# Moving stores, token sums and down-weight sums between the stages of a four-layer LoRA kernel, with five rank-table buffers

## The chip, the core and the metric

The kernel runs on one core of one Trainium2 chip. The metric is the device time in microseconds (us) of one execution. The core has five engines with a stream of instructions each: PE (matrix products; PEld is its weight load), DVE and ACT (elementwise work; both can read and write PSUM, where products arrive), POOL (elementwise work on SBUF, and indirect gathers), and SP, which here only issues transfers. ACT and POOL issue transfers too. Each stream is worked off in its order.

## The reference

Eight sequences of 256 tokens with 1024 features pass four layers, each added to its input. Every sequence b picks its own low-rank (rank 16) adapter in each layer.

```python
# layer 0: dense 1024 -> 1024 with bias, plus adapter times 2
x = x + (x @ W.T + b + 2.0 * (x @ A0[i0[b]]) @ B0[i0[b]])
# layer 1: gate and up 1024 -> 2752, silu, down 2752 -> 1024, adapters times 0.5 on all three
g = x @ W_gate.T + 0.5 * lora(x, A_gate, B_gate, i1[b])
u = x @ W_up.T   + 0.5 * lora(x, A_up, B_up, i1[b])
h = silu(g) * u
x = x + (h @ W_down.T + 0.5 * lora(h, A_down, B_down, i1[b]))
# layers 2 and 3: adapters alone
x = x + (x @ B2[i2[b]].T) @ A2[i2[b]].T
x = x + (x @ B3[i3[b]].T) @ A3[i3[b]].T
```

All of it is float32.

## The kernel before

The 2048 tokens are two blocks of 1024. Features lie on the 128 partitions, tokens along the free dimension. The large products use a seven-product scheme for 2 by 2 block matrices (seven products of sums of blocks in place of eight), once for layer 0 and for the last part of the down projection, and in two levels for the rest, where each of the seven outer products is again made of seven. So sums of weights and sums of tokens are needed next to each product: POOL makes most of the weight sums, DVE and ACT the token sums.

The work is a list of units, in this order: `layer0(0)` and `layer0(1)` with four units each; then for block 0 and after it for block 1 `gate_up` (first `rest()`, a group of leftover columns with seven short units, then five groups 0 to 4 of seven units), the two-level `Down` (seven units, called d_0 to d_6 below) and four units `2_blk_o` of the one-level down products. After the last of these, `last_layers()` applies layers 2 and 3 and stores the outputs. A unit has seven products and slots 0 to 9 between them. Other work is put in with `u.at(slot, f)`, or with `u.before(k, slot, f)` for a slot of the unit k places earlier. There is also a side queue, `beside`, of small work items with a cost: at each slot, items are taken from its front until their costs reach the unit's share. `need(key)` takes items until that key is done, so a unit that needs its token sums drains everything ahead of them.

This gives a program order. The framework then orders each engine's stream by its own planning of what is ready when, with program order as the priority, and sets the semaphores; tiles come from pools, and a load waits for a free tile of its pool.

Names that matter here:

- `upool` has 22 tiles of 1 MB (`big(...)`); nearly all weights, tokens and results lie in them.
- `apool` holds the gathered rank tables: `a0`, `agu` (two for each block, for the gate and up adapters, gathered by `shrink_tables` and copied into `w_r_B` by ACT at L1047), `bb` (for layers 2 and 3) and `a2s`.
- `prepare_tokens(blk, kk, h)` makes one half (kk) of the token sums of layer 1's outer products: four `inner` sets and two `outer_sums`, written to DRAM (`toks`). `load_tok` reads them back as `tk` (`tk_r` for the leftover group).
- `finished(kk)` in layer 0 stores layer 0's result to `x1d`, and calls `prepare_tokens` for block 0. For block 1 this is done later by `next_tokens`, which loads `x1d` as `xn`.
- `sum_down(c)`, c from 0 to 7, makes an eighth of the outer weight sums of the down projection (`wo` to `wsum`), once for both blocks, in POOL's stream.
- `Down.load_first` and `load_second` load a unit's weights (`dw_d`, `dx_d`, `db_d`) and tokens (`dh_d`, `dk_d`); `sum_weights` (POOL, L591 to L594) and `sum_tokens` (DVE and ACT, through PSUM tiles `pt_d`) make the inner sums.
- Results of the outer products are `c_X`, `c_E`, `c_Z`, `c_Y` (`c_d_` in the down stage, `c_r_` in the leftover group); DVE combines two of them at L496. `td` (L927) collects the down adapter's rank rows, and `pl` (L931) are the adapter products of gate and up.

Of the kernel before, what the change touches and what calls it, by code (L numbers as in the profile page):

```python
# [13 lines left out]
P = 128  # L14
# [10 lines left out]
NBLK = NB * S // TB  # L25
NN = TB // 512
# [26 lines left out]
def kernel(  # L53
# [50 lines left out]

    const = ctx.enter_context(tc.tile_pool(name="const", bufs=1))
    upool = ctx.enter_context(tc.tile_pool(name="u", bufs=NBIG))
    apool = ctx.enter_context(tc.tile_pool(name="a", bufs=3))
    adpool = ctx.enter_context(tc.tile_pool(name="ad", bufs=2))
    bpool = ctx.enter_context(tc.tile_pool(name="b", bufs=1))
    bgpool = ctx.enter_context(tc.tile_pool(name="bg", bufs=2))  # L110
# [521 lines left out]

    def prepare_tokens(blk, kk, h):


        t, items = {}, []

        def add(cost, f):
            items.append((cost, f))

        def outer():
            for n in ("sa", "sb"):
                t[n] = big(f"{n}_{blk}_{kk}").rearrange("p (i c t) -> p i c t", i=2, c=2)

        def outer_sums(c):
            a, b = ((h[n][:, 0, c], h[n][:, 1, c]) for n in range(NN))
            held = []

            def start():
                for x in (a, b):  # L650
                    held.append(bank(ps_l, f"pq_{blk}_{kk}_{c}_{len(held)}"))
                    copy(held[-1], x[0])

            def first():
                p1, p2 = held
                nc.vector.tensor_sub(t["sb"][:, 0, c], p1, b[0])
                nc.vector.tensor_add(p2, p2, b[1])

            def second():
                p1, p2 = held  # L660
                copy(t["sa"][:, 0, c], p2)
                nc.vector.tensor_sub(p1, p2, a[0])
                copy(t["sa"][:, 1, c], p1)
                nc.vector.tensor_sub(t["sb"][:, 1, c], a[1], p1)

            return (0, start), (1.4, first), (1.4, second)

        def inner(n, get, place, count):
            def start():
                b = get().rearrange("p i c (j t) -> p i (c j) t", j=2)  # L670
                t[n, "b"] = b
                t[n, "t"] = big(f"tt_{n}_{blk}_{kk}")[:, : count * 1024].rearrange(
                    "p (i s t) -> p i s t", i=count, s=4
                )
                nc.sync.dma_start(
                    out=toks[blk][place : place + count, kk, :, : 3 * S].rearrange("i p t -> p i t"),
                    in_=b[:, :, 1:4, :].rearrange("p i s t -> p i (s t)"),
                )
                b12, b11, b22, b21 = (b[:, :, j, :] for j in range(4))
                t[n] = token_sums(  # L680
                    f"pr_{n}_{blk}_{kk}",
                    b11,
                    b12,
                    b21,
                    b22,
                    *(t[n, "t"][:, :, j, :] for j in range(4)),
                    like=lambda ps: ps[:, : count * S].rearrange("p (i t) -> p i t", i=count),
                )

            def store():  # L690
                nc.sync.dma_start(
                    out=toks[blk][place : place + count, kk, :, 3 * S :].rearrange("i p t -> p i t"),
                    in_=t[n, "t"].rearrange("p i s t -> p i (s t)"),
                )
                ready.update((blk, k, kk) for k in range(place, place + count))

            cost = 0.84 if count == 1 else 1.4
            add(0, start)
            add(0, lambda: t[n][0]())
            add(cost, lambda: t[n][1]())  # L700
            add(cost, lambda: t[n][2]())
            add(0, store)

        inner("h0", lambda: h[0], 0, 2)
        split = len(items)
        add(0, outer)
        for c in range(2):
            items.extend(outer_sums(c))
        inner("sb", lambda: t["sb"], 4, 2)
        inner("sa", lambda: t["sa"], 2, 2)  # L710
        inner("h1", lambda: h[1][:, 1:2], 6, 1)
        return items[:split], items[split:]


    x1d = [
# [26 lines left out]
    def layer0(blk):  # L742
# [63 lines left out]
        def finished(kk):  # L806
            for n in range(NN):
                nc.sync.dma_start(
                    out=x1d[blk][n, kk], in_=st["x1", n, kk].rearrange("p i c t -> p (i c t)")
                )  # L810
            if blk == 0:
                for items in prepare_tokens(blk, kk, [st["x1", n, kk] for n in range(NN)]):
                    beside.extend(items)

        def plain(o, at):

# [64 lines left out]
        for i, o in enumerate((0, 2, 1, 3)):  # L881
            if blk == 0 and i == 0:
                u = Unit("0_plain", lambda at, o=o: plain(o, at), 0)
                u.before(1, 0, lambda o=o: load_w(o))
                u.before(1, 0, load_x)
                for c in range(HC):
                    u.before(1, 0, lambda c=c: sum_x(c))
            else:
                u = Unit(f"0_{blk}_{o}", lambda at, o=o: job(o, at), 1.3)
                u.before(1, 0, lambda o=o: load_w(o))  # L890
                u.before(1, 3, lambda o=o: sum_w(o))
                if i == 0:
                    u.before(1, 0, load_x)
                    for c in range(HC):
                        u.before(1, 4 + c // 2, lambda c=c: sum_x(c))
                    u.at(4, first_shrink)
            if i % 2:
                u.at(8, lambda kk=o % 2: finished(kk))

    def gate_up(blk):  # L900
        st = sts[blk]
# [38 lines left out]
        def job(g):  # L940
# [86 lines left out]
            q = Quads(blk, f"1_{blk}_{g}", 2, raw, done, SHARE)  # L1027
            q.units[0].before(3, 0, lambda: tables(g))
            if blk == 0 and g < KQ:
                for s, c in ((2, 2 * g), (5, 2 * g + 1)):  # L1030
                    q.units[s].at(4, lambda c=c: sum_down(c))

        def rest():

# [89 lines left out]
    def down_projection(blk):  # L1124
# [21 lines left out]

            queue(("x2", blk, mh, n), *((0.69, lambda k=k: add(k)) for k in range(HC)))

        Down(blk, f"d_{blk}", done)

        def load_h():
            st["h"] = []
# [154 lines left out]
        def last_layers():  # L1307
# [7 lines left out]
            for o in range(NC):  # L1315
# [3 lines left out]
                for n in range(NN):  # L1319
                    nc.vector.tensor_add(x2[o][n], x2[o][n], pss[n])  # L1320
                    at = blk * TB + n * 512
                    nc.scalar.dma_start(
                        out=outT[o * P : (o + 1) * P, at : at + 512], in_=x2[o][n]
                    )

        def next_tokens():

            parts = []
            for kk in range(2):
                h = []  # L1330
                for n in range(NN):
                    t = big(f"xn_{blk}_{n}_{kk}")
                    nc.sync.dma_start(out=t, in_=x1d[blk + 1][n, kk])
                    h.append(t.rearrange("p (i c t) -> p i c t", i=2, c=2))
                parts.append(prepare_tokens(blk + 1, kk, h))
            for part in zip(*parts):
                for items in part:
                    beside.extend(items)

        for o in range(HC):  # L1340
            u = Unit(f"2_{blk}_{o}", lambda at, o=o: job(o, at), 1.2)
            for g in (KQ, REST):
# [7 lines left out]
                u.before(2, 5, tables23)  # L1350
            else:
                u.at(5, lambda o=o: shrink23([o - 1, o - 1 + HC]))
            if o == 0 and blk + 1 < NBLK:
                u.at(3, next_tokens)
        units[-1].at(9, last_layers)

    for blk in range(NBLK):
# [148 lines left out]
```

## Time and profile before

| | us |
|---|---|
| median of 3 runs | 1838.62 |
| the three runs | 1838.72, 1838.62, 1835.54 |
| profiled execution | 1848.62 |
| its span, from the first to the last instruction | 1846.9 |

| engine | busy us | share of the span | instructions |
|---|---|---|---|
| PE | 1797.9 | 97% | 7588 |
| PEld | 1314.5 | 71% | 7588 |
| DVE | 1082.2 | 59% | 1674 |
| POOL | 1001.2 | 54% | 773 |
| ACT | 308.4 | 17% | 548 |

A row of the profile names the source line, the engine, the operation and the tiles, result first, without their numbers; what stands in brackets is the time that the engine stood idle before it and what ended that. The mean granted clock of PE is 0.989 of full speed. The stages lie in the trace as follows: layer 0 to 243 us, block 0's gate and up to about 768, its two-level down products to about 948, its one-level ones to about 1026, mixed with the first leftover products of block 1 from 1022 on; block 0's last layers end near 1048.

### The profile page before, as it was taken

The numbers are of one execution on the slowest core, as the hardware profiler recorded it, in microseconds if no ns is written. First come the engines' busy times: TensorE is split into PE (matmuls) and PEld (weight loads), VectorE is DVE, ScalarE is ACT, GpSimd is POOL, SyncE is SP. The second block draws the span as 40 slices with busy tenths as digits, with TensorE's granted clock in tenths as the row PEclk, the third lists the DMA queues.
The fourth block names the chain that finished last, engine by engine and source line by source line (L and its number), as shares of the span: only waits on it lengthen the run. The fifth ranks groups of instructions, "written<-read, shape, count | busy, mean of one in ns | idle before, by whom it ended". The sixth has DMA issues, their size and how long they took to land.

```text
span 1846.9 us, 20533 instructions
## 1 busy us (share of the span) xinstructions
PE 1797.9 (97%) x7588; PEld 1314.5 (71%) x7588; DVE 1082.2 (59%) x1674; ACT 308.4 (17%) x548; POOL 1001.2 (54%) x773
## 2 busy tenths in 40 slices
PE   7899999999999999999999699999999999999998
PEld 3344477878788878788864377888888887888843
DVE  3475235676857575755554564656565657456623
ACT  0112013111111112123112132020202030122100
POOL 5102067897988877453520568585858574344400
PEclk9999999999999999999999899999999999999999
DMA  6177466768686857573664884666666656555302
GB/s 225 77 256 297 157 280 235 278 214 313 222 307 239 309 198 266 200 252 120 218 256 142 313 357 152 231 228 231 227 231 230 229 198 243 205 195 179 113 0 91
DMA packets 114707, 402.33 MB, mean 218 GB/s; under 512 B 12336, under 2 KB 42160, under 8 KB 105136
## 3 DMA queue, kind: packets, MB, share of 16 engines
q1 hardware_dynamic: 97920, 362.84, 53.7%
q0 software_dynamic: 10208, 27.67, 4.3%
q10 hardware_dynamic: 6480, 10.51, 1.6%
q8 instruction: 61, 1.00, 0.2%
q14 instruction: 38, 0.31, 0.0%
HBM read 316.56 MB, written 84.41 MB: 217 GB/s over the span
## 4 chain that ended last, share of the span: by engine, by line
PE 88%; DVE 7%; DMA 2%; issue 1%; another core or an unknown queue 1%; POOL 0%; ACT 0%; ACTq 0%; DVEq 0%
PE pa L453 25%; PE pc L453 12%; PE pa_d L453 10%; PE pa L352 9%; PE pb L453 6%; PE pc_d L453 5%; PE pc L352 5%; PE pb_d L453 3%; PE pa_r L453 2%; PE pb L352 2%; PE pl L931 2%; PE pc_r L453 1%; DVE c_Y L496 1%; PE pd L238 1%
## 5 line engine op out<-in xcount | busy, mean ns | idle before, releaser
L453 PE MATMUL pa<-tk,sw 128*128 128x256 f32 x1120 | 270.6, 385 | 1.7 <-DVE c_X L484 1.7
L453 PE MATMUL pc<-tk,sw 128*128 128x256 f32 x1120 | 268.2, 383 | 0.0
L453 PEld LDWEIGHTS pa<-tk,sw 128*128 128x128 f32 x1120 | 210.2, 191 | 59.7 <-issue 14.0
L453 PEld LDWEIGHTS pc<-tk,sw 128*128 128x128 f32 x1120 | 214.8, 192 | 31.4 <-issue 1.6
L453 PE MATMUL pa<-tk,w_B 128*128 128x256 f32 x960 | 228.5, 381 | 0.4 <-DVE c_Y L487 0.4
L453 PEld LDWEIGHTS pa<-tk,w_B 128*128 128x128 f32 x960 | 181.2, 190 | 35.2 <-DVE c_E L484 6.5
L423 POOL TENSOR_TENSOR sw<-w_B 128x512 f32<-128x512 f32 x60 | 76.5, 1275 | 106.9 <-PE pa L453 87.0
L453 PE MATMUL pb<-tk,w_B 128*128 128x256 f32 x480 | 114.2, 381 | 0.0
L591 POOL TENSOR_TENSOR dx_d<-dw_d 128x1024 f32<-128x1024 f32 x14 | 33.4, 2387 | 143.5 <-PE pa L453 44.3
L453 PE MATMUL pa_d<-dh_d,dw_d 128*128 128x256 f32 x448 | 101.3, 379 | 0.0
L453 PE MATMUL pc_d<-dh_d,dw_d 128*128 128x256 f32 x448 | 101.3, 379 | 0.0
L453 PEld LDWEIGHTS pb<-tk,w_B 128*128 128x128 f32 x480 | 92.1, 192 | 12.8
L484 DVE TENSOR_TENSOR c_X<-c_X,pa 128x512 f32<-128x512 f32 x90 | 61.3, 681 | 63.7 <-PE pa L453 63.7
L414 POOL TENSOR_TENSOR w_B<-w_B,w_B 128x1024 f32<-128x1024 f32 x40 | 93.7, 2366 | 2.4 <-PE pa L453 2.4
L453 PEld LDWEIGHTS pa_d<-dh_d,dw_d 128*128 128x128 f32 x448 | 85.1, 190 | 11.6
L453 PEld LDWEIGHTS pc_d<-dh_d,dw_d 128*128 128x128 f32 x448 | 85.1, 190 | 11.6
L425 POOL TENSOR_TENSOR sw<-w_B 128x512 f32<-128x512 f32 x60 | 83.9, 1398 | 0.0
L426 POOL TENSOR_TENSOR sw<-w_B,sw 128x512 f32<-128x512 f32 x60 | 81.8, 1363 | 3.5
L424 POOL TENSOR_TENSOR sw<-sw,w_B 128x512 f32<-128x512 f32 x60 | 80.2, 1336 | 0.0
L263 ACT ACTIVATE c_X<-pa 128x512 f32<-128x512 f32 x30 | 17.8, 592 | 368.9 <-PE pa L453 332.6
L208 POOL DMA_INDIRECT ad<-in_ad_dram,off_a x48 | 45.6, 950 | 27.3 <-PE pd L238 16.4
L352 PE MATMUL pa<-ht,wd 128*128 128x512 f32 x128 | 59.3, 595 | 1.0 <-DVE c_d_Y L1225 1.0
(363 smaller groups left out, 3178.2 us busy)
## 6 DMA issues: line engine op xcount, KB each, us to landing
tk<-toks SPq DMA_DIRECT2D x140, 896.0 KB
w_B<-in_wgu_dram SPq DMA_DIRECT2D x40, 1024.0 KB
tk_r<-toks SPq DMA_DIRECT2D x28, 896.0 KB
hk<-c_Z SPq DMA_DIRECT2D x32, 512.0 KB
dh_d<-hk SPq DMA_DIRECT2D x14, 1024.0 KB
hk<-c_Y SPq DMA_DIRECT2D x24, 512.0 KB
w<-in_w_dram SPq DMA_DIRECT2D x16, 512.0 KB
x1d<-x SPq DMA_DIRECT2D x8, 1024.0 KB
```

The costliest lines, as they stand in the source:

```text
L208: nc.gpsimd.indirect_dma_start(out=t, out_offset=None, in_=table, in_offset=bass.IndirectOffsetOnAxis(ap=off, axis=0),)
L238: nc.tensor.matmul(ps[32 * r : 32 * r + 32, :], v, src, start=start, stop=stop, skip_group_check=True)
L352: nc.tensor.matmul(ps, v[j], m[j], start=start and k == 0, stop=k == len(moving) - 1, skip_group_check=True,)
L414: f(self.raw[out][:, c], self.raw[a][:, c], self.raw[b][:, c])
L423: nc.gpsimd.tensor_add(s1, m21, m22)
L424: nc.gpsimd.tensor_sub(s2, s1, m11)
L425: nc.gpsimd.tensor_sub(s3, m11, m21)
L426: nc.gpsimd.tensor_sub(s4, m12, s2)
L453: nc.tensor.matmul(ps[:, q, :], w(j, q, kk), tok(j, kk), start=start and q == 0 and kk == 0, stop=kk == self.deep - 1, skip_group_check=True,)
L484: nc.vector.tensor_add(view(out, r, k), view(old, r, k), ps)
L591: nc.gpsimd.tensor_sub(s3, a11, a21)
L931: nc.tensor.matmul(ps[outs], st["bgu", g][rows, table, n, cols], st["t"][rows, table, n, :], start=True, stop=True, skip_group_check=True,)
```

## The change

Five things are altered.

- The output stores of block 0 are no longer issued in `last_layers` right after each add; each becomes an item of cost 0.2 in the side queue, where units of block 1's leftover group take them. Block 1's stores stay where they were.
- `next_tokens` is no longer called at slot 3 of the first one-level down unit for both halves; it is called for one half at slot 0 of unit d_1 and for the other at slot 0 of unit d_3 of block 0's two-level down products.
- `prepare_tokens` returns one list in place of two; before, the two halves' lists were interleaved for block 1.
- `sum_down`: the first goes to slot 6 of the third unit of `layer0(1)`, the next two to slot 0 of the fourth, and the other five to groups 0, 0, 1, 1 and 2 of block 0 (two in each of groups 0 to 3 before).
- `apool` has five tiles in place of three.

```diff
-    apool = ctx.enter_context(tc.tile_pool(name="a", bufs=3))
+    apool = ctx.enter_context(tc.tile_pool(name="a", bufs=5))
...
         inner("h0", lambda: h[0], 0, 2)
-        split = len(items)
         add(0, outer)
...
-        return items[:split], items[split:]
+        return items
...
             if blk == 0:
-                for items in prepare_tokens(blk, kk, [st["x1", n, kk] for n in range(NN)]):
-                    beside.extend(items)
+                beside.extend(prepare_tokens(blk, kk, [st["x1", n, kk] for n in range(NN)]))
...
                 u.at(8, lambda kk=o % 2: finished(kk))
+            if blk == 1 and i > 1:
+                for c in ((0,), (1, 2))[i - 2]:
+                    u.at((6, 0)[i - 2], lambda c=c: sum_down(c))
...
             if blk == 0 and g < KQ:
-                for s, c in ((2, 2 * g), (5, 2 * g + 1)):
-                    q.units[s].at(4, lambda c=c: sum_down(c))
+                for s, c in ((2, 2 * g + 3), (5, 2 * g + 4)):
+                    if c < 8:
+                        q.units[s].at(4, lambda c=c: sum_down(c))
...
-        Down(blk, f"d_{blk}", done)
+        two = Down(blk, f"d_{blk}", done)
...
-                    nc.scalar.dma_start(
-                        out=outT[o * P : (o + 1) * P, at : at + 512], in_=x2[o][n]
-                    )
-
-        def next_tokens():
-
-            parts = []
+
+                    def store(o=o, n=n, at=at):
+                        nc.scalar.dma_start(
+                            out=outT[o * P : (o + 1) * P, at : at + 512], in_=x2[o][n]
+                        )
+
+
+                    if blk + 1 < NBLK:
+                        beside.append((0.2, store))
+                    else:
+                        store()
+
+        def next_tokens(kk):
+
+            h = []
+            for n in range(NN):
+                t = big(f"xn_{blk}_{n}_{kk}")
+                nc.sync.dma_start(out=t, in_=x1d[blk + 1][n, kk])
+                h.append(t.rearrange("p (i c t) -> p i c t", i=2, c=2))
+            beside.extend(prepare_tokens(blk + 1, kk, h))
+
+        if blk + 1 < NBLK:
             for kk in range(2):
-                h = []
-                for n in range(NN):
-                    t = big(f"xn_{blk}_{n}_{kk}")
-                    nc.sync.dma_start(out=t, in_=x1d[blk + 1][n, kk])
-                    h.append(t.rearrange("p (i c t) -> p i c t", i=2, c=2))
-                parts.append(prepare_tokens(blk + 1, kk, h))
-            for part in zip(*parts):
-                for items in part:
-                    beside.extend(items)
-
+                two.units[1 + 2 * kk].at(0, lambda kk=kk: next_tokens(kk))
...
-            if o == 0 and blk + 1 < NBLK:
-                u.at(3, next_tokens)
```

## The prediction

> **What bounds the kernel now.** I read the page first: PE is busy in 97% of the span and holds 88% of the chain of work that ended last, so only time in which PE stands, or runs at a lower granted clock, can be won. Of its 40 slices one in the middle stands out with a 6: the hand-over from block 0 to block 1. Stretches of 10 us show it, with one stretch of block 0's gate-up stage below them. The columns are PE, PEld, DVE, ACT and POOL busy time with counts, then granted clock, DMA share and GB/s.
>
> ```profile
> 1010.00:1020.00 10.00, 9.12 (x33) 3.31 (x31) 5.34 (x10) 4.84 (x9) 5.07 (x6) 1.00 0.25 86
> 1020.00:1030.00 10.00, 7.02 (x28) 2.48 (x28) 7.00 (x12) 2.67 (x5) 1.18 (x2) 1.00 0.86 309
> 1030.00:1040.00 10.00, 6.66 (x16) 3.18 (x17) 5.41 (x11) 1.74 (x4) 8.42 (x11) 0.70 0.88 316
> 1040.00:1050.00 10.00, 8.29 (x29) 3.98 (x27) 7.90 (x13) 0.00 (x0) 3.75 (x6) 0.96 1.03 370
> 1050.00:1060.00 10.00, 2.23 (x5) 1.85 (x6) 0.42 (x1) 0.77 (x2) 8.35 (x8) 0.73 1.03 375
> 1060.00:1070.00 10.00, 10.00 (x45) 8.65 (x44) 3.19 (x8) 1.40 (x4) 4.44 (x5) 0.93 1.00 390
> 660.00:670.00 10.00, 8.34 (x22) 5.49 (x20) 7.21 (x11) 0.00 (x0) 10.00 (x7) 0.66 0.83 308
> ```
>
> From 1010 to 1060 PE stands for 16.7 us (0.88 + 2.98 + 3.34 + 1.71 + 7.77). Next, the waits of PE tell who ended these stops (total, times, longest):
>
> ```profile
> PE pc_r L453 <- ACT c_r_X L263: 8.6, 1, 8.6
> ...
> PE pc_r L453 <- POOL sw_r L423: 2.6, 1, 2.6
> PE p L238 <- DVE pq L662: 1.7, 1, 1.7
> ...
> PE pa L352 <- DVE c_d_Y L1225: 1.0, 1, 1.0
> ```
>
> And the timeline tells what those engines were held by. ACT's copy came late because 16 output stores stood ahead of it in ACT's stream; POOL's sums stood behind table gathers that waited for a free buffer; SP took 17.74 us over six token loads.
>
> ```profile
> 1028.52 0.94 POOL L208 DMA_INDIRECT bb<-in_bb_dram,off_a  x1 [8.53 <-PE p L238]
> ...
> 1042.79 17.74 SPq L402 DMA_DIRECT2D tk_r<-toks  x6
> ...
> 1057.24 0.38 ACT L263 ACTIVATE c_r_X<-pc_r 128x256 f32<-128x256 f32 x1 [19.05 <-DMA out_dram<-c_d_Y]
> ...
> 1057.77 2.05 PE L453 MATMUL pc_r<-tk_r,sw_r 128*128 128x256 f32 x4 [8.55 <-ACT c_r_X L263]
> ```
>
> **The change, part by part.** Each gain below is PE standing time plus the clock lost around it.
>
> *Stores.* Before, each of 16 stores (256 KB) is issued by ACT right behind its DVE add; unhindered an issue takes 0.34 us, but from the ninth on ACT also waits for earlier transfers (the chain shows 4.41 us for one), so `c_r_X` comes 19.05 us late and PE stands 8.6 us. After, the stores are side items of cost 0.2 in the first remainder unit of block 1: its share is 0.5 per slot, so three go per slot and all 16 in six slots, with the unit's copies between them. A copy can still meet one waiting store: I leave half of the 4.41 us in the sum. Gain 8.6 - 2.2 = 6.4. If all stores are still ordered ahead of the copies, the gain is 0. The four result tiles (of 22) are freed a few us later; among the waits of SP's queue, token loads already waited 11.0 us for `out_dram<-c_d_Y`. What pays for that is the next part.
>
> *Token sums.* Per half (kk) this moves 20 DVE operations of 0.69 us and 4 of 0.42 = 15.5 us, 20 ACT copies (17 of about 0.6 us, 3 of 0.39: 11.4 us), and 10 transfers (two 1 MB loads, eight stores, 8.1 MB together; SP's issues take about 0.35 us each, 3.5 us). They leave 933 to 1040, where DVE's stream held PE by 1.7 and 1.0 us (the rows above) and 0.3 us more (`c_d_X` L1225), and go beside the down products d_1 and d_3. Gain 3.0. It also makes the first remainder tokens ready 100 us earlier, so that SP's 17.74 us of late loads has no part any more. The cost is in the down stage, where PE never stands now:
>
> ```profile
> 800.00:850.00 50.00, 50.00 (x236) 43.07 (x235) 26.86 (x37) 13.11 (x24) 23.03 (x12) 1.00 0.69 238
> 850.00:900.00 50.00, 50.00 (x234) 44.01 (x233) 27.64 (x40) 12.20 (x21) 19.53 (x13) 1.00 0.48 163
> ```
>
> DVE is busy 27 of 50 us. A down unit is 7 products of 3.45 us = 24.2 us, so DVE has 24.2 x 23/50 = 11 us free in it, and a half needs 15.5. The side queue is first-in first-out and each down unit drains it up to its own token sums: d_2's sums stand behind the whole half. If the half must fit into one unit, they are 4.5 us late, twice: 9 us. On SP, ahead of the second loads of unit d_2 and d_4, two 1 MB loads are put; at the page's mean of 218 GB/s that is 9.6 us, and ACT's first copy waits for them (7.5 and 9.6 us before, `pr_h <- DMA xn`); a PSUM product of 3.45 us covers only part. Bounds 0 and 13 with some clock; below 0 is excluded, since PE has no stop here to lose. I take 3, near the low end, because DVE stands as long as 16.7 us at a time in this stage (before its operation at 859.25), so work that is ready can run early.
>
> *Five rank-table buffers.* The trace has POOL standing 39.6 us before the second `agu` table (for the ACT copies of the first), 3.7 us before the first `bb` and 8.53 us before the second, for the last shrink products of block 0; `sw_r` stands behind that. With five, two `bb` and two `agu` tables of the hand-over fit at once and one is free; the next tables take `agu`'s place after its copies, not `bb`'s. Gain 2.6. The second `agu` gathers (4 of 1.25 us with issue) come about 90 us earlier, among the `wd` sums near 915; POOL stood 7.1 us there, which covers them; without that cover they cost up to 5. Below, the sums keep their durations.
>
> *Clock.* The granted clock was 0.70, 0.96, 0.73 and 0.93 in the four stretches from 1030: (0.30 x 6.7) + (0.04 x 8.3) + (0.27 x 2.2) + (0.07 x 10) = 3.6 us of PE's time, and it goes with the stops. So far 6.4 + 3.0 + 2.6 + 3.6 = 15.6. What stays: about 3.5 us of short stops in block 0's last layers (DVE `t`, `c_d_E`, `c_d_X`) and at `trep`. They are what is late next.
>
> *Down-weight sums.* A `sum_down` is 4 POOL operations of 1.28 us and 5 POOL DMA issues (0.8 and 4 of 0.56), 2 MB in all, in one tile. Eight run now in block 0's gate-up, two in each of four groups; of these the second of group 3 falls on DVE's crowded end:
>
> ```profile
> 655.77 1.28 POOL L423 TENSOR_TENSOR sw<-w_B 128x512 f32<-128x512 f32 x1
> 655.92 4.12 DVE L496 TENSOR_TENSOR c_Y<-c_Y,c_X 128x512 f32<-128x512 f32 x1
> ...
> 661.89 1.99 PE L931 MATMUL pl<-trep,bgu 32*128 32x512 f32 x2 [1.66 <-DVE td L927]
> ```
>
> The `wo` work delayed POOL's `sw` sums into DVE's add of two SBUF tiles, which took 4.12 us where it takes 0.69 alone; DVE's backlog then held PE 1.66 us, and the clock fell to 0.66 in that stretch (0.34 x 8.3 = 2.8). After, group 3 has none and group 2 only its first: gain 1.7 + 2.8 = 4.5. Here a rule speaks otherwise. The Trainium skill ("TensorE: Matmul & The Clock Gate", "The HAM clock gate") has the clock fall only after an idle window of about 3.4 us; by it this stop would cost 1.7 alone and the sum be 2.8 smaller. The row shows the loss after 1.66 us, with 22 matmuls where neighbours have 50, so I take 4.5 and keep 1.7 as the low end. Three sums go to block 1's layer 0 (about 211 to 243 us), where POOL stands 32 us for a buffer. There a rule speaks against the change: by "SBUF — State Buffer", "Who interferes with whom", a DVE operation with two SBUF inputs waits for a GpSimd operation that reads SBUF to finish, and layer 0's weight sums on DVE are of that kind. By the rule that is at most 1.28 us each, by the row above 3.4. DVE is busy 12.6 of 50 us from 200 to 250, so either is hidden. The three tiles are dearer: SP already took 24.4 us over four remainder-token loads at 197. Bounds 0 and 8, none below 0; I take 1, since four tiles of x come free in the same units.
>
> **Sum.** -15.6 - 4.5 + 3 + 1 = -16.1 us. The profiled execution took 1848.6 (span 1846.9), 10.0 above the median of 1838.62, so 1832.5 by its own time and 1822.5 by the median. With the bounds its own range is 1810 to 1831.
>
> **Rivals.** *The stores stay in the way.* The streams are ordered by the framework's planner, which already runs remainder products among the last down products; it may keep 16 stores together, or the kept result tiles may hold the token loads. Then 6.4 and the clock of the last two stretches (1.3) stay lost: -16.1 + 7.7 = -8.4, 1830. For: the stores are ready as soon as DVE is done, whatever their place in the program. Against: the copies would now come first in program order.
>
> *Tiles run out beside the down products: slower.* A down unit asks for 7 of the 22 tiles, and three units overlap, beside up to four result tiles. A half of the token sums asks for 8 more (2 loaded, 2 outer, 4 inner sums). Tiles come free at 7 per 24.2 us, one per 3.45 us. The lead of a unit's last load over its first reader:
>
> ```profile
> 833.80 0.32 SPq L585 DMA_DIRECT2D dk_d<-hk  x1
> ...
> 859.85 0.68 DVE L321 TENSOR_TENSOR dk_d<-dh_d,pt_d 128x512 f32<-128x512 f32 x1
> ```
>
> is 26 us, less some 5 us of transfer: 21. Six tiles held at once delay a load by 6 x 3.45 = 20.7, just within it; with eight it is 27.6 and PE stands 7 us per half. If the second half starts before the first has let go, up to sixteen delay it by 55 and PE stands about 34 us. From 24 us in the down stage the kernel is slower; 7 + 7 is not enough, an overlap is. A partial overlap (11 to 13 tiles, 17 to 24 us on top of one half's 7) gives 1838.6 - 19.1 + 28 = 1847.5; the full one 1853. For: loads already go out only when tiles come free, at the pace of the units. Against: the halves are two units (48 us) apart.
>
> **How the numbers follow.** The sum as worked out: 0.53. Stores still in the way: 0.18. Gains and down-stage cost about equal: 0.05. Tiles short: 0.24. Anything within 0.2% (3.7 us) counts as no change, about what a measurement of this kernel can tell. So faster 0.70, same 0.06 (it takes in a tail of the second case), slower 0.24. The range runs from 1806 (the remaining short stops gone too) to 1848 (through the partial overlap), which leaves out about 0.05 below and 0.12 above.
>
> **What would show it.** Right: no row of PE waiting for ACT `c_r_X` over 3 us, stores between ACT copies, no POOL wait of 39.6 us at `agu`, `xn` loads near 790 and 840, `tk_r` loads before 1000, clock 1.00 across the hand-over, no stop near 660. Wrong: PE below 49 of 50 us between 790 and 910 with `pa_d` or `pc_d` waiting for DVE `pt_d` or POOL `dw_d`; ACT standing behind stores as now; a stop at 243 to 300 for `tk_r`. A down stage longer by over 20 us would overturn the forecast.

## The result and the profile after

The changed kernel takes 1823.9 us (median of 19 runs, 1816.38 to 1836.04) against 1836.95 for the kernel before (19 runs beside it): ratio 0.9938, with a 95% interval of 0.9922 to 0.9954, so 8 to 14 us less (the ratio is taken over all timed runs; the two medians alone would give 0.9929). The profiled execution took 1823.25 us, span 1821.5.

The same stretches of 10 us around the hand-over (PE, PEld, DVE, ACT, POOL busy with counts, then granted clock, DMA share, GB/s), and the three stretches that the prediction showed of gate-up and down:

```profile
1010.00:1020.00 10.00, 10.00 (x35) 3.73 (x34) 2.58 (x4) 0.38 (x1) 0.00 (x0) 1.00 0.26 93
1020.00:1030.00 10.00, 9.75 (x37) 4.47 (x35) 7.56 (x14) 0.00 (x0) 0.21 (x1) 1.00 0.52 195
1030.00:1040.00 10.00, 9.33 (x39) 7.01 (x39) 5.47 (x12) 1.15 (x3) 7.95 (x7) 1.00 1.02 363
1040.00:1050.00 10.00, 9.14 (x43) 7.76 (x42) 2.80 (x7) 1.43 (x4) 8.10 (x10) 1.00 1.03 424
1050.00:1060.00 10.00, 10.00 (x48) 8.79 (x48) 5.16 (x12) 1.53 (x4) 9.84 (x12) 1.00 1.02 427
...
660.00:670.00 10.00, 10.00 (x50) 7.93 (x49) 7.88 (x13) 3.87 (x7) 8.59 (x8) 1.00 0.14 41
...
800.00:850.00 50.00, 49.70 (x229) 42.91 (x228) 37.89 (x57) 22.48 (x43) 19.57 (x8) 1.00 0.86 328
850.00:900.00 50.00, 42.81 (x190) 36.55 (x189) 44.50 (x61) 17.54 (x33) 22.45 (x13) 0.97 0.88 319
```

PE stands 1.8 us between 1010 and 1060, where it stood 16.7, and the clock is full. The stop near 660 is gone. In the down stage, where PE never stood, it now stands 7.2 of the 50 us from 850, with DVE busy 44.5 (27.6 before). PE's waits name it:

```profile
PE pc_d L453 <- DVE c_d_X L487: 5.7, 1, 5.7
PE pc_d L453 <- ACT dh_d L263: 1.8, 3, 1.1
...
PE pl L931 <- DVE td L927: 1.3, 1, 1.3
PE pa_r L453 <- ACT c_r_Z L263: 0.9, 1, 0.9
```

The 8.6 us for ACT `c_r_X` and the 2.6 for POOL `sw_r` are gone. A new wait of 5.7 us for DVE stands at their head.

The stages are cut at PE's first product of a kind: layer 0, the leftover group, group 0, the first two-level down product, the first one-level one ("hand-over" is from there to group 0 of block 1). What follows the hand-over, almost the whole of block 1, takes 740.1 to 742.9 us in all of them. Times in us, from one profiled execution each; "gate-up" is from group 0 to the down stage. The ratio is that of the timed runs to the kernel before that ran beside them.

| kernel | layer 0 starts | gate-up | down | hand-over | span | ratio (95%) |
|---|---|---|---|---|---|---|
| before | 56.6 | 477.6 | 171.3 | 165.3 | 1846.9 | |
| after | 46.6 | 469.3 | 181.7 | 146.4 | 1821.5 | 0.9938 (0.9922 to 0.9954) |
| c0 before again | 45.7 | 481.5 | 171.3 | 165.4 | 1841.5 | 1.0007 (0.9992 to 1.0021) |
| p1 buffers alone | 44.9 | 478.6 | 171.3 | 156.3 | 1829.8 | 0.9952 (0.9935 to 0.9969) |
| p2 stores alone | 45.7 | 480.7 | 171.3 | 165.5 | 1840.1 | 1.0001 (0.9986 to 1.0017) |
| p3 weight sums alone | 45.7 | 472.3 | 171.3 | 165.4 | 1828.9 | 0.9992 (0.9980 to 1.0004) |
| m1 without token sums | 45.9 | 476.7 | 171.4 | 159.2 | 1830.6 | 0.9939 (0.9918 to 0.9959) |
| m2 without buffers | 45.3 | 471.7 | 183.6 | 147.2 | 1826.4 | 0.9975 (0.9963 to 0.9988) |
| m3 without stores | 45.0 | 468.0 | 183.9 | 144.7 | 1818.4 | 0.9947 (0.9932 to 0.9962) |
| m4 without weight sums | 46.3 | 477.4 | 184.4 | 144.9 | 1829.7 | 0.9959 (0.9941 to 0.9976) |
| v1 second half later | 45.3 | 468.3 | 178.3 | 146.6 | 1816.2 | 0.9894 (0.9875 to 0.9912) |
| v2 rank rows earlier | 45.2 | 471.4 | 180.8 | 144.8 | 1819.1 | 0.9919 (0.9897 to 0.9942) |
| v3 buffers and weight sums | 46.5 | 473.1 | 171.3 | 154.3 | 1823.3 | 0.9923 (0.9905 to 0.9941) |
| v4 both halves late | 45.2 | 474.4 | 324.6 with the hand-over | | 1822.8 | 0.9935 (0.9919 to 0.9950) |

The first row is not to be read without the control. The profiled execution of before stood near the start, once:

```profile
40.00:50.00 10.00, 4.60 (x30) 1.26 (x22) 0.00 (x0) 0.00 (x0) 6.62 (x7) 1.00 0.13 41
50.00:60.00 10.00, 7.08 (x15) 2.84 (x16) 5.59 (x9) 1.20 (x2) 3.78 (x4) 0.66 0.09 26
...
PE pp L253 <- DVE t_s L231: 6.0, 1, 6.0
```

Layer 0 began 10 to 12 us later there than in every other kernel of the table, the control (the same code) among them; what caused that stop is open. So of the 25.4 us between the spans of before and after, 10.1 are chance. The other 15.3 are hand-over -18.9, gate-up with its leftover group -7.1, down +10.4 and 0.3 elsewhere.

How far can single profiles be trusted? "m3 without stores" answers it, for a reason given with that run: its engines' streams are those of the changed kernel, row for row. Its stages still differ from "after" by 1.3 us in gate-up, 2.2 in down and 1.7 in the hand-over. Up to the down stage m1 and v1 to v4 have these streams too, and their gate-up runs from 468.0 to 476.7 us. So a difference of 9 us in gate-up, or of 2 in the other two stages, between two profiles may be none.

### The profile page after: what moved, and what is told of

Read it like the earlier page. It is cut to its first block, busy times and chain, and to the rows that moved or that the text cites. A ratio compares the mean times of both kernels' runs of the same rounds, so it can differ in the third digit from the quotient of the medians.

```text
span 1821.5 us, 20497 instructions
## 1 busy us (share of the span) xinstructions
PE 1790.1 (98%) x7588; PEld 1310.4 (72%) x7588; DVE 1081.7 (59%) x1674; ACT 307.0 (17%) x548; POOL 1002.7 (55%) x773
## 4 chain that ended last, share of the span: by engine, by line
PE 91%; DVE 7%; DMA 1%; issue 1%; ACT 0%; DVEq 0%; SPq 0%; ACTq 0%
PE pa L453 26%; PE pc L453 13%; PE pa L352 10%; PE pa_d L453 9%; PE pb L453 6%; PE pc_d L453 5%; PE pc L352 5%; PE pb L352 3%; PE pb_d L453 2%; PE pl L931 2%; PE pa_r L453 2%; PE pp L822 2%; PE pd L238 1%; PE pc_r L453 1%; PE p L238 1%
## 5 line engine op out<-in xcount | busy, mean ns | idle before, releaser
L208 POOL DMA_INDIRECT ad<-in_ad_dram,off_a x48 | 45.9, 957 | 37.8 <-PE pd L238 27.1
L592 POOL TENSOR_TENSOR dw_d<-dw_d,db_d 128x1024 f32<-128x1024 f32 x14 | 34.4, 2460 | 45.4 <-DVE dk_d L321 12.6
```

What stands on the lines that cost most here:

```text
L208: nc.gpsimd.indirect_dma_start(out=t, out_offset=None, in_=table, in_offset=bass.IndirectOffsetOnAxis(ap=off, axis=0),)
```

## The experiments

**Control.** The kernel before, with no edit.

> The kernel before, unchanged, as a control. Of the 25.4 us between the two profiles, 10.1 lie before the second layer-0 unit (first product at 56.63 us before, 46.58 after), where none of the five edits works. Theory A (that part is chance of one execution): this run's profile starts that unit near 46.6 us and its span is near 1837. Theory B (the old order of the streams causes it): near 56 us again. Ratio 1.000 in either case.

1839.1 us beside 1837.35, ratio 1.0007. The stop at the start does not come back (45.7 us): theory A. The span is 1841.5 and not 1837, most of it in gate-up, 3.9 us longer than in the first profile. The hand-over is 165.4 as before.

**Each part alone.** Three of the five edits, put singly into the kernel before.

```diff
-    apool = ctx.enter_context(tc.tile_pool(name="a", bufs=3))
+    apool = ctx.enter_context(tc.tile_pool(name="a", bufs=5))
```

> Only the five rank-table buffers. Theory A (each part works in its own stage): the second agu table is gathered near 915 and not near 1007, no POOL wait of 39.6 us, PE's 2.6 us wait for sw_r goes; the stores and token sums still hold PE, so the hand-over (first one-level down product to first product of group 0 in block 1, 165.3 us before) shortens by about 3, ratio 0.998. Rival (the waits are in series, and freeing one only lets the next end later): under 1 us, ratio 1.000.

Five buffers alone take 0.48% off the time (1826.92 beside 1837.35). Among the stages it is the hand-over that is shorter beyond the scatter: 165.4 to 156.3, three times what theory A said. PE's stops from 1010 on, in the timeline of the control, were 15.9 us together; with five buffers they are 11.0. The stop for `sw_r` (2.57) and the two for DVE `c_d_E` L1225 (1.61) and `c_d_Y` (0.96) are gone. (How the buffers end the two DVE stops was not traced.) The rest of the 9.1 us is clock: the control has 0.86, 0.63, 0.89 and 0.60 in the four stretches from 1020, this kernel 1.00, 0.80, 0.68 and 1.00. The stop for `c_r_X` stays. From the timeline of this kernel:

```profile
998.15 0.97 POOL L208 DMA_INDIRECT bb<-in_bb_dram,off_a  x1 [39.61 <-ACT w_r_B L1047]
...
1040.66 2.05 PE L453 MATMUL pc_r<-tk_r,sw_r 128*128 128x256 f32 x4 [8.35 <-ACT c_r_X L263]
```

The 39.6 us of POOL's standing has not gone, though the prediction said so: it now stands before a `bb` table. But that table is gathered at 998, not at 1028.5, so `sw_r` behind it is in time. Nor do block 1's second `agu` gathers move to 915: both its `agu` tables are gathered already in layer 0, from 162 to 171 us, where the control has 903 to 907 and 1001 to 1005.

```diff
-                    nc.scalar.dma_start(
-                        out=outT[o * P : (o + 1) * P, at : at + 512], in_=x2[o][n]
-                    )
+                    def store(o=o, n=n, at=at):
+                        nc.scalar.dma_start(
+                            out=outT[o * P : (o + 1) * P, at : at + 512], in_=x2[o][n]
+                        )
+                    if blk + 1 < NBLK:
+                        beside.append((0.2, store))
+                    else:
+                        store()
```

> Only the stores moved into the side queue. Theory A: PE's 8.6 us wait for ACT's copy falls to under 3 and the hand-over shortens by 6 to 9 us, ratio 0.996. Rival (the 16 stores are still ordered together, and the next thing behind them, the late token loads, holds PE instead): the hand-over stays within 2 us of 165.3, ratio 1.000.

Nothing: ratio 1.0001, hand-over 165.5. The wait for `c_r_X` is only split (5.7 and 1.5 us): one copy now gets in after the eleventh store, the next only behind the fifteenth.

```diff
             if blk == 0 and g < KQ:
-                for s, c in ((2, 2 * g), (5, 2 * g + 1)):
-                    q.units[s].at(4, lambda c=c: sum_down(c))
+                for s, c in ((2, 2 * g + 3), (5, 2 * g + 4)):
+                    if c < 8:
+                        q.units[s].at(4, lambda c=c: sum_down(c))
...
+            if blk == 1 and i > 1:
+                for c in ((0,), (1, 2))[i - 2]:
+                    u.at((6, 0)[i - 2], lambda c=c: sum_down(c))
```

> Only the down-weight sums moved. Theory A: block 0's gate-up stage (first leftover product to first two-level down product, 525.2 us before) shortens by 4 to 7 us, no stop in its fourth group, layer 0 within 1 us; hand-over and down stage unchanged; ratio 0.997. Rival (the stop only moves to another place in the gate-up stage, or layer 0 pays for it): gate-up and layer 0 together within 2 us, ratio 1.000.

The profiled gate-up stage is 9.2 us shorter than the control's, but the timed gain is 0.08% (-0.04 to 0.20), so not resolved. The two profiles mislead: the control's execution took 4.1 us more than the median of its kernel (1843.22 and 1839.1), this one 4.9 less (1830.68 and 1835.6). Over all profiles of the table, gate-up takes 471.7 us on average with the weight sums moved (nine kernels, 468.0 to 476.7) and 479.2 without (five, 477.4 to 481.5). The two groups do not overlap, so the direction is plain. Of the 7.5 us between the means, an estimated 4.7 are again the choice of execution: against their own medians the nine profiles are 1.3 us short on average and the five 3.4 long (the stop at the start of before taken off). That leaves about 3 us.

**Each part taken out of the changed kernel.**

```diff
-                two.units[1 + 2 * kk].at(0, lambda kk=kk: next_tokens(kk))
...
+            if o == 0 and blk + 1 < NBLK:
+                u.at(3, next_tokens)
```

(Not shown: `prepare_tokens` and `next_tokens` are again those of the kernel before, with the two halves' lists interleaved.)

> The changed kernel with the token sums put back to the first one-level down unit (stores, weight sums and five buffers as changed). Stages of the changed kernel: two-level down 181.7, hand-over 146.4, gate-up of block 0 518.1 with the leftover group. Theory A (moving the token sums costs 10 us in the down stage and brings about as much or more at the hand-over): down 171.3, hand-over 155 to 160, ratio 0.993 to 0.996. Rival (the token sums bring nothing that five buffers do not bring already): hand-over within 3 us of 146.4 and the kernel 8 to 10 us faster than the changed one, ratio near 0.989.

The time is that of the changed kernel (0.9939 against 0.9938). So the token sums, the largest move of the change, bring nothing in sum that the timed runs resolve: the hand-over is 12.8 us longer without them and the down stage 10.3 shorter. Of the 12.8, 7.7 are stops of PE (10.4 against 2.6 us in the stage) and the rest is clock; v3 below, with the token sums as late and stops of 10.2 us, has a hand-over of 154.3. How they shorten the stops is seen in the stores. In this kernel ACT's 16 stores (and its copy between them) take from 1019.61 to 1039.3. From its timeline (rows in a chain are merged: "x10" counts loads up to 1053):

```profile
1019.61 0.35 ACTq L1328 DMA_DIRECT2D out_dram<-c_d_E  x1
1027.13 25.94 SPq L402 DMA_DIRECT2D tk_r<-toks  x10
1038.81 0.39 ACT L263 ACTIVATE c_r_X<-pa_r 128x256 f32<-128x256 f32 x1 [7.44 <-DMA out_dram<-c_d_Z]
1039.25 2.08 PE L453 MATMUL pa_r<-tk_r,sw_r 128*128 128x256 f32 x4 [5.68 <-ACT c_r_X L263]
```

And in the changed kernel, where the tokens came earlier:

```profile
972.39 37.05 SPq L402 DMA_DIRECT2D tk_r<-toks  x4
...
1024.03 0.35 ACTq L1325 DMA_DIRECT2D out_dram<-c_d_E  x1
...
1033.36 0.52 ACTq L1325 DMA_DIRECT2D out_dram<-c_d_Y  x1
1033.93 0.38 ACT L263 ACTIVATE c_r_X<-pa_r 128x256 f32<-128x256 f32 x1 [15.06 <-DMA out_dram<-c_d_Y]
1035.53 0.38 ACT L263 ACTIVATE c_r_X<-pa_r 128x256 f32<-128x256 f32 x1 [1.22 <-PE pa_r L453]
```

The stores are still in one block ahead of all but one of ACT's copies, so the edit of the stores did not spread them. But the block lasts 9.9 us in place of 19.7 (21.2 in the kernel before). The adds that feed it are not the reason: DVE is done with the sixteenth after 9.0 us here and 10.2 there, and the last store goes out 0.4 and 9.1 us behind it. What lies beside the block differs. In m1 SP issues two stores of token sums (1020.21 and 1022.07) and then two of the ten token loads (1027.13 and 1028.95; the next comes at 1039.33), and ACT's stores land 4.2 to 10.6 us after their issue. In the changed kernel SP issues nothing from 1009.5 to 1031.77, when 13 of the 16 are out; the first twelve land after 2.1 to 3.5 us (the last four, beside three loads, after 6.0 to 13.8), and no issue takes over 0.60 us. That the token sums' transfers stretch the block is thus read from the order in time; no run moves these transfers alone. ACT's 15.06 us of standing costs PE no wait for `c_r_X`: PE is in the `p<-t,a` products of the last layers until 1031.75.

```diff
-    apool = ctx.enter_context(tc.tile_pool(name="a", bufs=5))
+    apool = ctx.enter_context(tc.tile_pool(name="a", bufs=3))
```

> The changed kernel with three rank-table buffers. With five buffers alone the hand-over fell from 165.4 to 156.3. Theory A (what they free is POOL's and ACT's order at the hand-over, needed by early tokens too): hand-over 155 or more, ratio 0.997 to 1.000. Rival (once the tokens are early, the tables' wait is off the path): hand-over within 3 us of 146.4, ratio near 0.994.

The ratio rises to 0.9975, outside the changed kernel's interval. But the profiled hand-over is 147.2 against 146.4, so with the token sums moved the buffers no longer act there. The profile puts the difference into the down stage (+1.9) and gate-up with its leftover group (+3.4), where single executions of the same streams differ by as much. Only POOL's stream differs at all between the two kernels. Where the buffers' timed gain lies in the changed kernel stays open.

```diff
-                    if blk + 1 < NBLK:
-                        beside.append((0.2, store))
-                    else:
-                        store()
+                    store()
```

> The changed kernel with block 0's stores issued at once again. Moving the stores alone gave 165.5 against 165.4: nothing, since the transfers ahead of ACT's copies and the loads behind them stayed late. Theory A (with the tokens already there the stores no longer matter either: they are ordered together in the changed kernel too): hand-over within 3 us of 146.4, ratio 0.994. Rival (only with the tokens early do the stores hold PE): a wait of PE for ACT's c_r_X of 5 us or more, hand-over 152 or more, ratio 0.997.

Ratio 0.9947 against 0.9938, with overlapping intervals, and a hand-over of 144.7. There was nothing to measure: in the two traces the instructions of PE, DVE, ACT, POOL and SP, with the tiles' names, follow each other in the same order from start to end. With the tokens early, the planner puts the stores in the same places with and without the edit. So this run is a second measurement of the changed kernel, and a test of nothing else. In the kernel before, the edit changes the order a little (p2) and the time not.

```diff
-                for s, c in ((2, 2 * g + 3), (5, 2 * g + 4)):
-                    if c < 8:
-                        q.units[s].at(4, lambda c=c: sum_down(c))
+                for s, c in ((2, 2 * g), (5, 2 * g + 1)):
+                    q.units[s].at(4, lambda c=c: sum_down(c))
...
-            if blk == 1 and i > 1:
-                for c in ((0,), (1, 2))[i - 2]:
-                    u.at((6, 0)[i - 2], lambda c=c: sum_down(c))
```

> The changed kernel with the down-weight sums as before. Alone they gave 0.9992 (0.998 to 1.0004), though block 0's gate-up was 477.6 and 481.5 us in the two profiles of before and 472.3 in theirs (first product of group 0 to first two-level down product). Theory A (they save 4 to 7 us there): this stage 476 to 481, ratio 0.996 to 0.998. Rival (the saving is within the scatter of this stage): ratio 0.9935 to 0.9945.

Ratio 0.9959 against 0.9938 (and 0.9947 of m3), overlapping; gate-up 477.4 against 469.3. The direction is that of p3; by the timed runs the size is again not resolved.

**What holds PE in the down stage.** Of the 10.4 us that this stage loses, 7.5 are stops and 2.9 clock. The changed kernel's timeline before the 5.7 us stop:

```profile
874.52 2.36 POOL L594 TENSOR_TENSOR dw_d<-dx_d,dw_d 128x1024 f32<-128x1024 f32 x1
874.68 3.28 DVE L1185 TENSOR_TENSOR rr<-rr 32x1024 f32<-32x1024 f32 x1
876.83 3.33 POOL L591 TENSOR_TENSOR dx_d<-dw_d 128x1024 f32<-128x1024 f32 x1
878.64 2.08 DVE L1186 TENSOR_TENSOR rr<-rr 32x512 f32<-32x512 f32 x1
882.11 2.77 POOL L592 TENSOR_TENSOR dw_d<-dw_d,db_d 128x1024 f32<-128x1024 f32 x1 [1.94 <-DMA db_d<-in_wd_dram]
882.72 2.72 DVE L1186 TENSOR_TENSOR rr<-rr 32x512 f32<-32x512 f32 x1
886.21 5.17 PE L453 MATMUL pc_d<-dh_d,dw_d 128*128 128x256 f32 x16 [5.72 <-DVE c_d_X L487]
```

The adds of rank rows (L1185, L1186: both inputs in SBUF) take 3.28, 2.08 and 2.72 us, where the same forms take 1.22 and 0.68 alone. Subtract those from each one's end, and the adds begin at 876.74, 880.04 and 884.76; POOL's sums end at 876.88, 880.16 and 884.88. So each add waits for one POOL operation to end. (An add of the same form at 880.75, when POOL stands, takes 1.22.) The excess is 5.5 us, and the stop 5.7. In the kernel before the same adds run at 869 to 873 and take 1.22 and 0.68. POOL's sums meet the rank rows because they are late. One waited 13.3 us on `toks<-sb`, a store that had to free a tile. Two versions try this.

```diff
-                u.before(3, 4, rank_rows)
+                u.before(5, 4, rank_rows)
```

> The changed kernel with the rank rows (DVE's adds of two SBUF tiles, 3.28, 2.08 and 2.72 us at 875 to 885 in place of 1.22 and 0.69) put from unit d_4 to unit d_2. Theory A (the 5.7 us stop near 880 is DVE's queue behind these adds, which POOL's late weight sums slow): the stop goes, down stage 174 to 177, ratio 0.990 to 0.992. Rival (tiles held by the token sums make loads late, and DVE's row is only the last to wait): a stop of 4 us or more stays in the down stage, now for POOL or a load, stage over 179, ratio 0.993 to 0.995.

The stop at 886 is gone and another stands at 835.7:

```profile
831.00 2.80 POOL L591 TENSOR_TENSOR dx_d<-dw_d 128x1024 f32<-128x1024 f32 x1 [2.10 <-DMA dh_d<-hk]
831.63 3.25 DVE L1186 TENSOR_TENSOR rr<-rr 32x1024 f32<-32x1024 f32 x1
835.74 5.32 PE L453 MATMUL pc_d<-dh_d,dw_d 128*128 128x256 f32 x16 [4.83 <-DVE c_d_Z L487]
```

The down stage stays at 180.8 and the ratio's interval (0.9897 to 0.9942) overlaps the changed kernel's. Theory A's ratio came out, its stage time did not. A stop of over 4 us stays, as the rival said, though again for DVE and not for POOL or a load: the adds took their wait along to where DVE was as full.

```diff
-            for kk in range(2):
-                two.units[1 + 2 * kk].at(0, lambda kk=kk: next_tokens(kk))
+            two.units[1].at(0, lambda: next_tokens(0))
...
+            if o == 0 and blk + 1 < NBLK:
+                u.at(3, lambda: next_tokens(1))
```

> The changed kernel with only the first half of the token sums at d_1; the second goes to slot 3 of the first one-level down unit, where both were before. Theory A (the second half is what the down stage cannot take: its DVE and tile load meets the rank rows and late POOL sums near 880): down stage 172 to 176 against 181.7, hand-over up to 150, ratio 0.988 to 0.991. Rival (the first half costs as much, or the hand-over needs both halves early): down over 178 or hand-over over 155, ratio 0.993 or more.

1817.47 us beside 1838.66, ratio 0.9894 (0.9875 to 0.9912): below the changed kernel's interval, and m3's. The hand-over keeps its gain (146.6), the down stage pays 6.9 in place of 10.4. So the ratio is theory A's, and the down stage, at 178.3, just the rival's. The 3.4 us saved there are less than half of the 8 us between the two ratios; the other part shows in no stage that this edit touches and stays unexplained. What is left there is the first half, and of the same kind:

```profile
822.48 2.68 POOL L594 TENSOR_TENSOR dw_d<-dx_d,dw_d 128x1024 f32<-128x1024 f32 x1
822.87 6.18 DVE L1147 TENSOR_TENSOR c_d_E<-c_d_E,x 128x512 f32<-128x512 f32 x3
825.83 2.67 POOL L591 TENSOR_TENSOR dx_d<-dw_d 128x1024 f32<-128x1024 f32 x1 [0.67 <-issue]
829.80 6.68 PE L453 MATMUL pc_d<-dh_d,dw_d 128*128 128x256 f32 x16 [2.90 <-DVE c_d_Z L487]
...
820.00:830.00 10.00, 7.10 (x33) 5.95 (x33) 9.86 (x8) 2.34 (x5) 7.72 (x3) 0.95 1.03 415
830.00:840.00 10.00, 10.00 (x34) 8.27 (x35) 4.64 (x8) 1.60 (x4) 7.04 (x3) 0.71 0.93 349
```

Three adds of 0.68 us (they add x to a result and are not part of the moved work) took 6.18 beside two POOL sums, PE stood 2.90, and the clock of the next stretch was 0.71.

```diff
-            two.units[1].at(0, lambda: next_tokens(0))
+            two.units[5].at(0, lambda: next_tokens(0))
```

> The stores, five buffers and weight sums as in the changed kernel; the second half of the token sums at slot 3 of the first one-level unit as in v1, and the first half at slot 0 of d_5 in place of d_1. Theory: the down stage pays because DVE, loaded with a half, meets POOL's weight sums of the next units; beside d_5 and d_6 only one set of those is left, so the stage from the first two-level to the first one-level down product is 171 to 174 us (181.7 changed, 178.3 in v1), while the hand-over stays at 145 to 149 us: span 1808 to 1813, ratio about 0.987. Rival 1: the stop goes with the half wherever it is put, as in v2: stage 176 to 180, ratio as v1, 0.989. Rival 2: both halves are now so late that the hand-over has its stops again: one-level stage above 153 us, ratio 0.992 or more.

This edit is against v1. The theory failed: the ratio is 0.9935 and not 0.987. Here one-level products run among the last two-level ones (cut as in the table, the stages would be 161.0 and 163.6 us), so only both stages together can be compared: 324.6 us, and 324.8 in v1 (328.2 after, 336.6 before). The first half's price has not gone; it stands elsewhere, now by DVE's load alone (its adds there are 0.69 us each):

```profile
910.00:920.00 10.00, 6.97 (x49) 4.42 (x48) 9.96 (x20) 4.39 (x9) 3.80 (x4) 0.86 0.51 188
920.00:930.00 10.00, 7.59 (x23) 3.91 (x22) 9.98 (x19) 6.00 (x12) 0.00 (x0) 0.97 0.95 348
```

In these stages that is the first rival; the time is what the second said, but not for its reason. The timed ratio is worse than v1's, with intervals apart. The profile puts 6.0 of the 6.6 us between the two spans into gate-up, although the streams of all engines are the same in both kernels until d_1, and identical streams scatter by as much there. So the timed difference between v1 and v4 stays unexplained, and with it how much of v1's lead over the changed kernel is due to its edit.

**Two parts without the others.** Five buffers and the weight sums, in the kernel before.

```diff
-    apool = ctx.enter_context(tc.tile_pool(name="a", bufs=3))
+    apool = ctx.enter_context(tc.tile_pool(name="a", bufs=5))
...
-                for s, c in ((2, 2 * g), (5, 2 * g + 1)):
+                for s, c in ((2, 2 * g + 3), (5, 2 * g + 4)):
...
+            if blk == 1 and i > 1:
+                for c in ((0,), (1, 2))[i - 2]:
+                    u.at((6, 0)[i - 2], lambda c=c: sum_down(c))
```

> Only the five buffers and the moved down-weight sums; stores and token sums as before. Theory A (these two carry the whole gain, while the token sums give back in the down stage what they bring at the hand-over): hand-over 156 to 160, down 171.3, ratio 0.992 to 0.995, as the changed kernel. Rival (the stores add to it once the buffers are five): 2 us or more worse than the kernel with the stores too, ratio 0.9955 or more.

Ratio 0.9923, within the changed kernel's interval; hand-over 154.3 and down 171.3, together 325.6 us against 328.2 in the changed kernel. The gain of the whole change is had with these two parts, most of it with the buffers (p1); stores and token sums as placed add nothing to it.

## Why the prediction was right, and where not

The total held: 1822.5 forecast, 1823.9 measured, and it was right to take off 10.0 us for the odd profiled execution of before (10.1 turned out to be its start). As a change it is 13.1 us where 16.1 were forecast; 1.7 of the difference come from the kernel before, which takes 1836.95 over 19 runs and not the 1838.62 of three. But the total owes much to luck: its terms were off in both directions, and their errors nearly cancel. The "own range" of 1810 to 1831 does not follow from the bounds given: those of the down stage and of layer 0 alone make it 1818.5 to 1839.5.

- *Stores, -6.4.* Failed as a term of its own. The stores alone bring 0, and the planner kept them together, as the first rival said. The stop did go, and as far as the times of issue and landing tell, because the token sums took away the transfers that stretched the block of stores from 9.9 to about 20 us. The prediction saw that ACT "waits for earlier transfers" and did not ask whose. Its row of six token loads in 17.74 us is a merged one: two go out before the stores are done and four behind them.
- *Token sums, -3.0.* With the stores' stop they take 7.7 us of stops out of the hand-over, 12.8 with the clock (m1 against after).
- *Five buffers, -2.6.* Mis-sized: alone 9.1 us of the stage and 8.8 of the time (0.48% of 1837), since DVE stops put down to token sums and some 4 us of clock went with them. The cost of up to 5 us, weighed for `agu` gathers near 915, had no object: those gathers moved to layer 0. In the profile of the changed kernel the buffers act no more in the hand-over.
- *Clock, -3.6.* Right in place: 1.00 from 1010 to 1060. Hand-over as a whole: -15.6 forecast, -18.9 measured.
- *Weight sums, gate-up, -4.5.* The stop near 660 went as said. The size was probably too large: the two profiles say -8.3 in the groups and +1.2 in the leftover group, but about 3 us are left when the profiles are set against their own medians, and the timed run of this part alone says 1.5 and at most 3.7.
- *Layer 0, +1.* 0.7 (186.7 after, 186.0 in the control; p3 and m4 show the same two values).
- *Down stage, +3.* The term that failed most: 10.4, inside its bounds of 0 to 13, near the upper one. The half was costed at its undisturbed durations, with DVE's standing time as cover. What was missing is that DVE's adds of two SBUF tiles wait there for POOL's sums of 2.4 to 3.3 us, and that clock goes with the stop (7.5 us of stops, 2.9 of clock). The rule that the prediction cited for layer 0 (the Trainium skill, "SBUF — State Buffer", "Who interferes with whom": such an operation waits until the GpSimd operation ends) is what the trace shows here, to within 0.15 us, and it should have been applied to this stage.
- *Tiles run out.* Did not decide. A tile made POOL's sums late by 13.3 us, but the stage lost 10.4 us and not 24.

The signs named for "right" came mostly true: no `c_r_X` row, full clock, no stop near 660, no POOL wait of 39.6 us at `agu`, the first `tk_r` loads before 1000 (934) and loads of `xn` early (760 and 820). Not true: stores between ACT's copies. And PE below 49 of 50 us in the down stage, named as a sign of "wrong", was there too, though it waited for DVE `c_d_X` and not for `pt_d` or `dw_d`; the limit that would have overturned the forecast, 20 us, was not reached.

## What to carry to other kernels

Before moving vector work to a stage where the vector engine "has time", count its operations that read two SBUF tiles beside GpSimd's sums: each can take on the rest of a GpSimd operation, and that cover is not free. When a queue's issues look slow, ask which transfers run beside them before moving the issues: with the token sums' transfers out of the way the block of stores halved, while moving the stores did nothing. Look whether an edit changes the engines' streams at all before reading its time. One profile with an odd stop can hold more than the change is worth; profile the old kernel twice, and set each profile beside the median of its own runs, before taking stages apart.

## What the runs showed of the hardware

The granted clock is lost in portions. Cut into 2 us, the stretches after v4's stop of 0.92 us for `td` (row at 369.11 of its timeline) show it:

```profile
369.11 1.12 PE L932 MATMUL pl<-trep,bgu 32*128 32x512 f32 x2 [0.92 <-DVE td L928]
...
368.00:370.00 2.00, 1.08 (x5) 0.29 (x2) 1.97 (x4) 0.00 (x0) 2.00 (x3) 1.00 0.98 298
370.00:372.00 2.00, 2.00 (x7) 1.54 (x7) 2.00 (x3) 0.00 (x0) 2.00 (x2) 0.77 1.09 416
372.00:374.00 2.00, 2.00 (x6) 1.62 (x5) 2.00 (x4) 0.00 (x0) 2.00 (x2) 0.50 1.03 434
374.00:376.00 2.00, 2.00 (x9) 1.71 (x9) 0.78 (x2) 0.00 (x0) 2.00 (x2) 0.88 0.72 291
```

The clock reaches 0.50, and the loss is 2 x (0.23 + 0.50 + 0.12) = 1.7 us: half speed for 3.4 us. After the changed kernel's stop of 5.72 us the stretches from 884 on have 0.94, 0.50 and 0.70: one such portion again, 1.7 us. After v1's stop of 2.90 us it is twice that, 2 x (0.24 + 0.50 + 0.50 + 0.47) = 3.4 us:

```profile
828.00:830.00 2.00, 0.20 (x1) 0.23 (x2) 2.00 (x3) 1.63 (x3) 0.51 (x1) 0.76 1.02 408
830.00:832.00 2.00, 2.00 (x5) 1.62 (x6) 2.00 (x5) 0.00 (x0) 1.19 (x1) 0.50 1.03 412
832.00:834.00 2.00, 2.00 (x6) 1.57 (x5) 1.95 (x4) 0.00 (x0) 1.92 (x2) 0.50 1.02 408
834.00:836.00 2.00, 2.00 (x6) 1.57 (x6) 0.00 (x0) 0.00 (x0) 1.92 (x2) 0.53 1.06 436
```

But v1's stop of 1.82 us, close to the place where v4 stood 0.92, costs nothing:

```profile
365.94 1.99 PE L453 MATMUL pa<-tk,w_T 128*128 128x256 f32 x8 [1.82 <-DVE c_X L487]
...
368.00:370.00 2.00, 2.00 (x9) 0.60 (x10) 1.97 (x4) 0.00 (x0) 2.00 (x2) 1.00 0.91 313
370.00:372.00 2.00, 2.00 (x10) 1.77 (x11) 2.00 (x4) 0.00 (x0) 2.00 (x3) 1.00 1.08 444
```

Nor does the changed kernel's stop of 1.29 us for the same `td` as in v4:

```profile
370.00:372.00 2.00, 0.71 (x3) 0.29 (x2) 1.97 (x5) 0.00 (x0) 2.00 (x3) 1.00 0.94 280
372.00:374.00 2.00, 2.00 (x9) 1.48 (x9) 2.00 (x2) 0.00 (x0) 2.00 (x2) 1.00 1.09 412
```

The rule weighed in the prediction (the Trainium skill, "TensorE: Matmul & The Clock Gate", "The HAM clock gate") fits in the half clock and in the portion of about 3.4 us, and not in the trigger: 0.92 us of idling was enough once, and 1.29 and 1.82 were not at other times. The same section says that its window runs freely; whether it matters where in it a stop falls, no run here tests. For a sum it means that a short stop costs itself and then 0, 1.7 or 3.4 us more, by chance as far as these rows tell. That is enough to make stages of single executions differ by some us. It shows in whole executions too: the changed kernel's shortest run (1816.38 us) has a mean granted clock of 0.996, its longest (1836.04 us) 0.989.
